# Attention ahead of an int8 linear layer: another order of the work before the first scores

## The chip, the cores and the metric

The kernel runs on one core of a Trainium2 chip. The metric is device time in microseconds (us), from the launch of the program to its end. Engines are TensorE (PE in the profile; its weight loads are PEld), VectorE (DVE), ScalarE (ACT), GpSimd (POOL) and SyncE (SP), which issues the DMA transfers. On-chip data lies in SBUF; matmuls write to PSUM, which has eight banks of 128 x 512 float32.

## What is computed

The input x has 8 batches of 512 channels by 1024 tokens; cond is a 0/1 mask of 8 x 1024. First comes masked self-attention with 16 heads of 32 channels, then a linear layer with int8 weights along the token axis, quantised by row, and the residual:

```python
Q, K, V = (proj(Wq), proj(Wk), proj(Wv))            # einsum 'oc,bct->bto', split into heads
att = einsum('bhqd,bhkd->bhqk', Q, K) / sqrt(32) + b[0]
att = softmax(att * m + (1 - m) * -1e30, axis=-1)   # m: the mask of the key
y = einsum('bhqk,bhkd->bhqd', att, V)               # back to (B, C, T)
scale = max(abs(y).max(-1), 1e-7) / 127
q = clip(round(y / scale), -128, 127).astype(int8)
out = x + (q @ weight.T * scale * w_scale + bias).astype(float16)
```

## The kernel before, in words

**Tiling.** Four heads (128 channels) of one batch are a group `i`; there are 32 groups. The 1024 tokens of the queries are two halves `h` of 512; a group and a half are `X` (64 of them). The keys go in eight chunks of 128. One step `s` of the main loop takes one X and one chunk: `scores(s)` (L408 on) computes the transposed scores of four heads into two PSUM tiles, ScalarE takes their exponentials (L433), GpSimd adds them up over the chunks (L445), and `product(s)` multiplies by v (L458). Scores are shifted by each query's largest score. The shift is the first operand that goes into a scores tile: a matmul of a block of ones with the tile `shift` (L419), after which the score matmuls accumulate (L424).

**Where the shift comes from.** One X ahead, `maxima(k)` computes the scores the other way round: one matmul pair per unit, a unit `k` being one X, one of four heads `j` and one of four blocks of 128 queries (16 units an X). VectorE reduces the 128 x 1024 result to one column (`take_maxima`, L376). The operands of these matmuls are stacks: 128 x 1024 tiles with the high and low parts of one head's q or k in four slabs of 32 rows, filled by DMA (`stack_head`, L322; four transfers of 64 KB for one head, one of q and k, and one half). When the 16 units of an X are reduced, `split_tops` (L395, L397, GpSimd) splits the column into three bfloat16 parts, and `place_tops` (L402) transposes them by DMA into `shift`.

**PSUM.** Pool `ps_s` (tag "s") has two tiles of two banks, used by the scores and by some maxima; `ps_m` (tag "m") one tile of two banks, for the other maxima; `ps_av` (tag "av") one bank for the product with v; `ps_job` (tag "job") one bank for projections and the linear layer. A tile is written again when its readers are done. `maxima_bank(k)` takes "s" for k mod 4 of 1 and 2, "m" for 0 and 3.

**The order.** It is written out by hand: each engine executes in program order, without a scheduler. The main loop runs over pairs of steps, `n`, with `i, p = divmod(n, 8)`. It starts at n = FIRST = -5; the pairs below 0 have no scores and prepare the first X. In each pair, `job(i, p)` returns a list of pieces of other matmul work (a projection of a later group, v, or the linear layer of an earlier one), which are dealt out between four maxima units, `jobs["bank"]` being the PSUM tile that they write. Where a pair has eight pieces, one of them is done as narrow matmuls (`columns`, L197) between the pair's two scores. What follows a pair (`flush(later)`, then `after_units`) stands behind it on the engines' streams: the low parts of q and k on VectorE, and the transfers on SP.

**Ahead of the pairs.** `first_projections` (L251 to L277) computes k of group 0 in a whole "s" tile, and q's first half in the "job" bank, chunk by chunk of the channels as x arrives; then it copies them to `full`, and makes high (ScalarE) and low parts (GpSimd). The first eight units are done from `full` by `first_maxima`, two units (heads 0 and 1) at a time (L363), in pairs -5 and -4. Units from 8 on need the stacks of heads 2 and 3, and X = 1 (units from 16, in pair -1) those of head 0 with q's second half.

The jobs of the pairs below 0, and what follows each:

| pair | job (eight pieces each) | stacks put on SP behind it, or at its start |
| --- | --- | --- |
| -5 | v of group 0, first half of the tokens | heads 2, then 3: k both halves, q first half |
| -4 | q of group 0, second half | head 0: k both halves, q second half |
| -3 | v of group 0, second half | |
| -2 | q of group 1, first half | |
| -1 | k of group 1, first half | at its start, behind the transpose: head 1 k both halves, heads 1, 2, 3 q second half |

The lines of pairs 1 and 2 (group 0, p = 1 and 2) in `job` give a quarter of v of group 1 each, four pieces; the linear layer of an earlier group, which fills these pairs later on, does not exist yet.

Of the kernel before, what the change touches and what calls it, by code (L numbers as in the profile page):

```python
# [9 lines left out]
F32 = mybir.dt.float32  # L10
# [10 lines left out]
P = 128  # L21
DH = 32
HG = P // DH
HALF = 512
QUARTER = 256
# [7 lines left out]
def kernel(  # L33
# [216 lines left out]

    def first_projections():  # L251

        pair = ps_s.tile([P, NH, HALF], F32, tag="s", name="kps_0")
        accs = [(1, 0, pair[:, 0, :]), (1, 1, pair[:, 1, :]), (0, 0, bank("qps_0"))]
        for c in range(NG):
            for which, h, acc in accs:
                nc.tensor.matmul(
                    acc,
                    w_qk[0, which][:, c, :],
                    x_sb[0, c][:, h * HALF : (h + 1) * HALF],  # L260
                    start=(c == 0),
                    stop=(c == NG - 1),
                )
        top = masks[0][1]
        for which, h, acc in accs:
            split_tiles(0, which, h)
            f = full[0, which, h]
            if which == 0:
                nc.scalar.activation(f, acc, AF.Copy, scale=top)
            elif h == 0:  # L270
                nc.vector.tensor_copy(f, acc)
            else:
                nc.scalar.copy(f, acc)
        for which, h, acc in accs:
            high, low = splits[0, which, h]
            nc.scalar.copy(high, full[0, which, h])
            nc.gpsimd.tensor_tensor(low, full[0, which, h], high.bitcast(F32), ALU.subtract)  # L277

    v_sb = {}

    def project_v(i, quarters):

        b, g = divmod(i, NG)
        KQ = QUARTER // P

        def piece(a, r, matmul=nc.tensor.matmul):
            if i not in v_sb:
                v_sb[i] = work.tile([P, NT, P], F32, tag="v", name=f"v_{i}", bufs=2)
            acc = jobs["bank"]
            t, part = divmod(r, 2)  # L290
            k = a * KQ + t
            place = (k - quarters[0] * KQ) * P
            for c in range(part * NG // 2, (part + 1) * NG // 2):
                matmul(  # L294
                    acc[:, place : place + P],
                    x_sb[b, c][:, k * P : (k + 1) * P],
                    wv_sb[:, c, g * P : (g + 1) * P],
                    start=(c == 0),
                    stop=(c == NG - 1),
                )  # L300
            if (a, r) == (quarters[-1], 2 * KQ - 1):
                nc.scalar.copy(  # L302
                    v_sb[i][:, quarters[0] * KQ : (a + 1) * KQ, :].rearrange("p k c -> p (k c)"),
                    acc[:, : place + P],
                )

        return [lambda *x, a=a, r=r: piece(a, r, *x) for a in quarters for r in range(2 * KQ)]
# [5 lines left out]
            [P, T], F32R, tag="qk"[which], name=f"{'qk'[which]}s_{i}_{j}"  # L313
        )

    def stack_head(i, j, which, h):
        order = ((0, 0, 1, 1), (0, 1, 0, 1))[which]
        if (i, j, which) not in stacks:
            stack_tile(i, j, which)
        s = stacks[i, j, which]  # L320
        for a, part in enumerate(order):
            nc.sync.dma_start(  # L322
                s[a * DH : (a + 1) * DH, h * HALF : (h + 1) * HALF].bitcast(F32),
                splits[i, which, h][part][j * DH : (j + 1) * DH, :].bitcast(F32),
            )
# [3 lines left out]

    def maxima_bank(k):  # L330

        pool, tag = (ps_s, "s") if k % HN in (1, 2) else (ps_m, "m")
        return pool.tile([P, NH, HALF], F32, tag=tag, name=f"mps_{k}")

    def maxima(k):
# [351 lines left out]
    def group(i):  # L687
        return 0 <= i < n_groups

    def job(i, p):  # L690


        if i == last:
            return linear(i - 2, p, (0,), HALF) if p < 2 else []
        if i < 0:
            if p in (3, 5):
                return project_v(0, (0, 1) if p == 3 else (2, 3))
            if p == 4:
                return project(0, 0, 1)
            return project(1, p - 6, 0)  # L700
        if p == 0:
            return project(i + 1, 1, 1)
        if p == 3:
            return project_v(i + 1, (2, 3))
        if p == 4:
            return project(i + 1, 0, 1)
        if p == 7:
            return project(i + 2, 1, 0) if group(i + 2) else []
        h, a = divmod({1: 0, 2: 1, 5: 2, 6: 3}[p], 2)
        pieces = linear(i - 2, h, (a,)) if group(i - 2) else []  # L710
        if p in (1, 2):
            pieces += project_v(i + 1, (a,))
        elif group(i + 2):
            pieces += project(i + 2, 0, 0, (a,))
        return pieces

    def after_units(i, p):

        flush(stores)
        if i == last:  # L720
            if p == 2:
                for step in range(5):
                    normalise(2 * i - 1, step)
            if p == 3:
                quantise(i - 1, 0)
            if p == 5:
                turn(i - 1)
                for step in range(5):
                    normalise(2 * i, step)
        elif group(i - 1):  # L730
            if p in (2, 3):
                normalise(2 * i - 1, 2 * p - 4)
                normalise(2 * i - 1, 2 * p - 3)

            if p == 4:
                normalise(2 * i - 1, 4)
            if p == 5:
                quantise(i - 1, 0)
            if p == 7:
                turn(i - 1)  # L740
        if group(i) and i < last:
            if p == 6:
                normalise(2 * i, 0)
                normalise(2 * i, 1)
            if p == 7:
                normalise(2 * i, 2)
        if p == 0 and group(i - 1):
            normalise(2 * i - 2, 3)
            normalise(2 * i - 2, 4)
        if i < 0 and p == 3:  # L750
            for which in (1, 0):
                for j in range(HG):
                    stack_tile(0, j, which)
            load_w(1, 1)
            for j in (2, 3):
                for which, h in ((1, 0), (1, 1), (0, 0)):
                    stack_head(0, j, which, h)
        if group(i + 1):
            b, g = divmod(i + 1, NG)
            if g == NG - 2 and p == 6 and b + 1 < B:  # L760
                load_mask(b + 1)
            if g == NG - 1 and b + 1 < B:
                if 1 <= p < 4:
                    prepare_mask(b + 1, p - 1)
                if p == 3:
                    load_x(b + 1, 0)
                if p == 4:
                    for c in range(1, NG):
                        load_x(b + 1, c)
        if p == 4 and group(i + 1):  # L770
            if group(i + 2):
                load_w(i + 2, 0)

            if i >= 0:
                for which, h in ((1, 0), (0, 0), (1, 1)):
                    stack_head(i + 1, HG - 1, which, h)
            for j in range(HG if i >= 0 else 1):
                if i < 0:
                    for h in range(NH):
                        stack_head(0, j, 1, h)  # L780
                stack_head(i + 1, j, 0, 1)
        if p == 1 and i >= 0 and group(i + 2):
            load_w(i + 2, 1)

        ahead = i + 1 + (p == 7)
        if p in (7, 0) and group(ahead) and ahead > 0:
            j = (0, 1)[p == 0]
            stack_head(ahead, j, 1, 0)
            stack_head(ahead, j, 0, 0)
            for j in {7: (), 0: (0, 1)}[p]:  # L790
                stack_head(ahead, j, 1, 1)
# [22 lines left out]
    for n in range(FIRST, n_pairs):  # L814
# [7 lines left out]
        if (n + 1) % HP == 0 and 0 <= n + 1 < n_pairs:  # L822
            split_tops((n + 1) // HP)
            place_tops((n + 1) // HP)
            if n == -1:
                for h in range(NH):
                    stack_head(0, 1, 1, h)
                for j in range(1, HG):
                    stack_head(0, j, 0, 1)
            if p == HN - 1 and i >= 0 and group(i + 1):  # L830
                for which, h in ((1, 0), (0, 0), (1, 1)):
                    stack_head(i + 1, 2, which, h)
# [17 lines left out]
        if p in (5, 6) and 0 <= i < last:  # L850
            half_denominators(2 * i, p - 5)
        if pieces:
            jobs["bank"] = bank(f"job_{n}")
        if n == n_pairs - 1:
            open_linear(last - 1, 1)
            run_linear(2)
# [20 lines left out]
        for a in range(HN):  # L877
# [3 lines left out]
            elif units:  # L881
                maxima(units[a])

            if a > 0 or len(pieces) > NG:
                for _ in range(-(-len(pieces) // (HN - a))):
                    pieces.pop(0)()
        flush(later)
# [64 lines left out]
```

## Time and profile before

| what | value |
| --- | --- |
| median of 3 runs | 2558.18 us (2558.08 to 2558.53) |
| the profiled execution | 2559.6 us |
| its span | 2557.8 us |
| TensorE busy in the span | 2506.1 us (98%) |
| GpSimd | 2242.7 us (88%) |
| VectorE | 1802.7 us (70%) |
| ScalarE | 1479.1 us (58%) |
| the first maxima matmul | 19.37 us from the span's start |
| the first scores matmul (pair 0) | 56.40 us |
| start of pair 1 | 67.51 us |

Times of instructions are counted from the start of the span. A line of the timeline gives start, length, engine, source line, operation, the tiles written and read, shapes and count, and in brackets how long the engine was idle before and what ended that. A line of the stages gives the stretch, its length, each engine's busy time (and count), the clock granted to TensorE, the share of the DMA engines' time, and GB/s. A busy TensorE is not the same as one at its peak, since matmuls are pipelined. An idle engine costs nothing where another one sets the end.

### The profile page before, as it was taken

The numbers are of one execution on the slowest core, as the hardware profiler recorded it, in microseconds if no ns is written. First come the engines' busy times: TensorE is split into PE (matmuls) and PEld (weight loads), VectorE is DVE, ScalarE is ACT, GpSimd is POOL, SyncE is SP. The second block draws the span as 40 slices with busy tenths as digits, with TensorE's granted clock in tenths as the row PEclk, the third lists the DMA queues.
The fourth block names the chain that finished last, engine by engine and source line by source line (L and its number), as shares of the span: only waits on it lengthen the run. The fifth ranks groups of instructions, "written<-read, shape, count | busy, mean of one in ns | idle before, by whom it ended". The sixth has DMA issues, their size and how long they took to land.

```text
span 2557.8 us, 50828 instructions
## 1 busy us (share of the span) xinstructions
PE 2506.1 (98%) x19425; PEld 1429.6 (56%) x19428; DVE 1802.7 (70%) x2893; ACT 1479.1 (58%) x1657; POOL 2242.7 (88%) x909
## 2 busy tenths in 40 slices
PE   7999999999999999999999999999999999999997
PEld 4555555555555555555555555555555555555532
DVE  4567677777777677776777777777677777777774
ACT  2556665565655555655656655566655566556554
POOL 1889899999999989998999999999999998999991
PEclk9999999999999999999999999999999999999999
DMA  4423433333333333334333343333433334333321
GB/s 129 107 69 80 119 76 82 82 104 98 90 79 93 105 82 89 79 93 109 82 84 95 81 118 77 80 85 94 114 84 75 85 96 109 84 82 80 80 70 44
DMA packets 225952, 228.09 MB, mean 89 GB/s; under 512 B 104368, under 2 KB 138160, under 8 KB 225712
## 3 DMA queue, kind: packets, MB, share of 16 engines
q1 hardware_dynamic: 225712, 224.85, 34.4%
q8 instruction: 156, 2.56, 0.4%
q14 instruction: 84, 0.69, 0.1%
HBM read 57.70 MB, written 16.78 MB: 29 GB/s over the span
## 4 chain that ended last, share of the span: by engine, by line
PE 79%; POOL 11%; DMA 3%; issue 2%; ACT 2%; DVE 1%; SPq 1%; POOLq 0%; DVEq 0%; ACTq 0%
PE mps L345 17%; PE av L458 15%; PE sps L424 14%; PE job L208 13%; POOL sum L445 10%; PE job L294 7%; PE sps L419 6%; PE job L635 3%; PE dps L474 2%; PE job L197 2%; DMA wq<-in_wqT 2%; ACT e L433 1%; DVE rest L376 1%; SPq L322 1%; DMA ks<-kl 1%
## 5 line engine op out<-in xcount | busy, mean ns | idle before, releaser
L445 POOL TENSOR_TENSOR sum<-sum,e 128x2048 f32<-128x2048 f32 x374 | 1706.7, 4563 | 39.1 <-ACT e L433 20.5
L376 DVE CUSTOM_DVE_ANT_0 rest<-mps,row 128x1024 bf16<-128x1024 f32 x1024 | 1254.2, 1225 | 620.0 <-PE mps L345 376.9
L433 ACT ACTIVATE e<-sps,kbias 128x1024 f32<-128x1024 f32 x1024 | 1085.8, 1111 | 453.7 <-PE sps L424 448.7
L345 PE MATMUL mps<-ks,qs 128*128 128x512 f32 x2032 | 764.9, 457 | 11.6 <-ACT e L433 8.1
L424 PE MATMUL sps<-qf,kf 32*128 32x512 f32 x4096 | 552.2, 590 | 0.0
L458 PE MATMUL av<-e,v 128*32 128x512 f32 x4096 | 493.4, 598 | 0.0
L345 PEld LDWEIGHTS mps<-ks,qs 128*128 128x128 f32 x2032 | 333.5, 190 | 238.8 <-DVE den L484 93.6
L445 POOL TENSOR_TENSOR sum<-e,e 128x2048 f32<-128x2048 f32 x63 | 286.2, 4542 | 154.8 <-ACT e L433 147.6
L458 PEld LDWEIGHTS av<-e,v 128*32 128x32 f32 x4096 | 107.5, 109 | 346.4 <-issue 346.1
L294 PEld LDWEIGHTS job<-wv,x 128*128 128x128 f32 x1860 | 255.0, 191 | 27.1
L208 PE MATMUL job<-x,wq 128*128 128x256 f32 x914 | 247.9, 380 | 10.8 <-DMA wq<-in_wqT 7.0
L294 PE MATMUL job<-wv,x 128*128 128x128 f32 x1860 | 257.1, 274 | 0.0
L419 PE MATMUL sps<-shift,ones_b 32*128 32x512 bf16 x2048 | 232.7, 383 | 5.9 <-DVE tops L376 3.0
L511 DVE RECIPROCAL den<-den 128x128 f32<-128x128 f32 x256 | 228.4, 925 | 0.0
L208 PE MATMUL job<-x,wk 128*128 128x256 f32 x854 | 223.8, 378 | 0.0
L424 PEld LDWEIGHTS sps<-qf,kf 32*128 32x128 f32 x4096 | 207.6, 184 | 4.3
L208 PEld LDWEIGHTS job<-x,wq 128*128 128x128 f32 x914 | 172.2, 189 | 47.7 <-DMA ks<-kl 8.4
L302 ACT COPY v<-job 128x256 f32<-128x256 f32 (+1 forms) x93 | 41.3, 444 | 252.5 <-PE job L294 252.5
L208 PEld LDWEIGHTS job<-x,wk 128*128 128x128 f32 x854 | 161.1, 189 | 30.9
L419 PEld LDWEIGHTS <-ones_b 32*128 32x128 bf16 x2048 | 70.6, 91 | 187.2 <-issue 169.6
L237 ACT ACTIVATE qh<-job,top 128x256 fp32r<-128x256 f32 (+1 forms) x91 | 49.8, 547 | 188.7 <-PE job L208 166.4
L635 PE MATMUL job<-w_sb,qT 128*128 128x256 bf16 (+1 forms) x942 | 125.9, 275 | 0.1
(101 smaller groups left out, 1438.4 us busy)
## 6 DMA issues: line engine op xcount, KB each, us to landing
ks<-kh SPq DMA_DIRECT2D x512, 64.0 KB, 2.0
ks<-kl SPq DMA_DIRECT2D x512, 64.0 KB, 2.0
qs<-qh SPq DMA_DIRECT2D x508, 64.0 KB, 2.0
qs<-ql SPq DMA_DIRECT2D x508, 64.0 KB, 2.0
x<-in_x SPq DMA_DIRECT2D x32, 512.0 KB, 6.0
xr<-in_x SPq DMA_DIRECT2D x64, 256.0 KB, 3.4
out<-o SPq DMA_DIRECT2D x64, 256.0 KB, 3.4
wk<-in_wkT SPq DMA_DIRECT2D x32, 256.0 KB, 3.7
```

Of the source, the lines that this page charges most:

```text
L197: nc.tensor.matmul(acc[r : r + DH], weights[:, r : r + DH], moving, **kwargs)
L208: matmul(acc[:, place], w[:, c, :], x_sb[b, c][:, h * HALF : (h + 1) * HALF][:, cols], start=(c == 0), stop=(c == NG - 1),)
L294: matmul(acc[:, place : place + P], x_sb[b, c][:, k * P : (k + 1) * P], wv_sb[:, c, g * P : (g + 1) * P], start=(c == 0), stop=(c == NG - 1),)
L345: nc.tensor.matmul(acc[:, a, :], q[:, n0 * P : (n0 + 1) * P], kk[:, a * HALF : (a + 1) * HALF], start=True, stop=True,)
L376: nc.vector.tensor_tensor_reduce(out=rest, in0=acc.rearrange("p h t -> p (h t)"), in1=row, scale=-1.0, scalar=HIGH, op0=ALU.add, op1=ALU.m ...
L419: nc.tensor.matmul(accs[j // 2][:, j % 2, :], ones_b[r, :], shift[r, :], start=True, stop=False)
L424: nc.tensor.matmul(accs[j // 2][:, j % 2, :], k[r, k0 * P : (k0 + 1) * P], q[r, :], start=False, stop=True,)
L433: nc.scalar.activation(e[:, 2 * a : 2 * a + 2, :], acc, AF.Exp, bias=kbias[:, kc : kc + 1], scale=SCALE)
L445: nc.gpsimd.tensor_tensor(sums[X], other, exps[s], ALU.add)
L458: nc.tensor.matmul(accs_av[X][r, :], v_sb[i][:, kc, r], exps[s][:, j, :], start=(kc == 0), stop=(kc == NT - 1),)
L511: nc.vector.reciprocal(piece, piece)
L635: matmul(acc, qT[:, k, :], w8_sb[:, k, half][:, cols], start=(k == 0), stop=(k == NT - 1),)
```

## The change

All of it lies ahead of pair 3.

- `first_projections` takes two "s" tiles, one for each half of k, in place of one. In the last chunk of channels, q's matmul comes first; ScalarE scales q before it copies k's second half.
- `maxima_bank`: units 0 to 19 (the pairs below 0) go by k mod 3: "m" for 1, "s" for 0 and 2, so the three tiles come round in turn.
- The jobs of the pairs below 0: q's second half over pairs -5 and -4, four pieces each, in one bank; v's first half in pair -3; group 1's q and k in -2 and -1 as before. v's second half is dealt to pairs 1 and 2, a quarter each, in the upper half of the bank (the `offset`) ahead of group 1's quarter. In the pairs below 0 a piece also follows the first of the four units in each case.
- The bank of these jobs is the "av" tile in pairs -3 and -1, the "job" tile otherwise.
- The stacks of head 3 are issued by ScalarE instead of SP. Head 0's k stack goes behind pair -5 on SP; head 1's k stack behind pair -4, after q's second half of head 0, in place of the start of pair -1.

```diff
-        pair = ps_s.tile([P, NH, HALF], F32, tag="s", name="kps_0")
-        accs = [(1, 0, pair[:, 0, :]), (1, 1, pair[:, 1, :]), (0, 0, bank("qps_0"))]
-        for c in range(NG):
-            for which, h, acc in accs:
+        k0, k1 = (ps_s.tile([P, HALF], F32, tag="s", name=f"kps_0_{h}") for h in range(NH))
+        accs = [(0, 0, bank("qps_0")), (1, 0, k0), (1, 1, k1)]
+
+        order = [(c, a) for c in range(NG - 1) for a in accs[1:] + accs[:1]]
+        order += [(NG - 1, a) for a in accs]
+        for c, (which, h, acc) in order:
...
-        for which, h, acc in accs:
+        for which, h, _ in accs[1:] + accs[:1]:
             high, low = splits[0, which, h]
...
-    def project_v(i, quarters):
+    def project_v(i, quarters, offset=0):
...
-            place = (k - quarters[0] * KQ) * P
+            place = offset + (k - quarters[0] * KQ) * P
...
-    def stack_head(i, j, which, h):
+    def stack_head(i, j, which, h, engine=nc.sync):
...
-        pool, tag = (ps_s, "s") if k % HN in (1, 2) else (ps_m, "m")
+
+        first = k < -FIRST * HN
+        pool, tag = (ps_s, "s") if (k % 3 != 1 if first else k % HN in (1, 2)) else (ps_m, "m")
...
         if i < 0:
-            if p in (3, 5):
-                return project_v(0, (0, 1) if p == 3 else (2, 3))
-            if p == 4:
-                return project(0, 0, 1)
-            return project(1, p - 6, 0)
+            if p < HP + 1:
+
+                if p == HP - 1:
+                    jobs["first"] = project(0, 0, 1)
+                return [jobs["first"].pop(0) for _ in range(NG)]
+            return project_v(0, (0, 1)) if p == 5 else project(1, p - 6, 0)
...
         if p in (1, 2):
+            if i == 0:
+
+                pieces = project_v(0, (NH + a,), QUARTER)
             pieces += project_v(i + 1, (a,))
...
-            for j in (2, 3):
+            for j, engine in ((2, nc.sync), (3, nc.scalar)):
                 for which, h in ((1, 0), (1, 1), (0, 0)):
-                    stack_head(0, j, which, h)
+                    stack_head(0, j, which, h, engine)
+            for h in range(NH):
+                stack_head(0, 0, 1, h)
...
             for j in range(HG if i >= 0 else 1):
-                if i < 0:
-                    for h in range(NH):
-                        stack_head(0, j, 1, h)
                 stack_head(i + 1, j, 0, 1)
+            if i < 0:
+                for h in range(NH):
+                    stack_head(0, 1, 1, h)
...
             if n == -1:
-                for h in range(NH):
-                    stack_head(0, 1, 1, h)
                 for j in range(1, HG):
                     stack_head(0, j, 0, 1)
...
         if pieces:
-            jobs["bank"] = bank(f"job_{n}")
+
+            if n < 0 and n % 2 and n > FIRST:
+                jobs["bank"] = ps_av.tile([P, HALF], F32, tag="av", name=f"job_{n}")
+            elif n != FIRST + 1:
+                jobs["bank"] = bank(f"job_{n}")
...
-            if a > 0 or len(pieces) > NG:
+            if a > 0 or len(pieces) > NG or n < 0:
                 for _ in range(-(-len(pieces) // (HN - a))):
                     pieces.pop(0)()
```

## The prediction

> **What bounds the kernel now.** I read the page first, then busy time by stage, then the timeline up to 100 us, the waits in it and the DMA issues.
>
> ```profile
> span 2557.8 us, 50828 instructions
> ...
> PE 2506.1 (98%) x19425; PEld 1429.6 (56%) x19428; DVE 1802.7 (70%) x2893; ACT 1479.1 (58%) x1657; POOL 2242.7 (88%) x909
> ...
> PE   7999999999999999999999999999999999999997
> ```
>
> TensorE is busy nearly everywhere: work on it costs its time, and only idle stretches can be won. They lie in the first slice, which is the stage that the change edits. By stage (the edges are the pairs' first matmuls; -5 and -4, then -3 to -1, then one pair a row from 0):
>
> ```profile
> core 0: us, PE busy (x) PEld busy (x) DVE busy (x) ACT busy (x) POOL busy (x), PEclk, DMA share, GB/s
> 19.37:36.47 17.10, 15.61 (x80) 9.32 (x80) 9.86 (x16) 2.81 (x6) 3.72 (x3) 1.00 0.36 87
> 36.47:56.40 19.93, 17.29 (x88) 14.08 (x89) 15.53 (x25) 2.39 (x4) 1.22 (x5) 1.00 0.31 79
> 56.40:67.51 11.11, 8.51 (x55) 5.16 (x56) 5.15 (x10) 5.32 (x6) 4.26 (x1) 1.00 0.40 97
> 67.51:76.76 9.25, 8.71 (x65) 4.62 (x64) 5.29 (x8) 5.32 (x6) 5.89 (x3) 1.00 0.67 189
> 76.76:86.17 9.41, 8.91 (x67) 4.74 (x67) 4.94 (x9) 4.62 (x5) 9.41 (x4) 1.00 0.47 122
> 86.17:97.11 10.94, 10.11 (x93) 6.52 (x93) 6.16 (x11) 5.20 (x6) 10.57 (x8) 1.00 0.22 54
> 97.11:106.90 9.79, 9.79 (x72) 5.61 (x73) 4.03 (x9) 4.72 (x5) 7.46 (x3) 1.00 0.35 89
> ```
>
> Pair 0 takes 11.11 us with 8.51 busy. VectorE has 9.86 and 15.53 us of work in 17.10 and 19.93. The timeline says where the chain waits:
>
> ```profile
> 27.95 1.99 PE L363 MATMUL mps<-kf,qf 32*128 32x512 f32 x8 [0.71 <-DVE tops L376]
> ...
> 36.47 0.73 PE L345 MATMUL mps<-ks,qs 128*128 128x512 f32 x2 [0.77 <-DVE tops L376]
> ...
> 48.45 1.23 DVE L376 CUSTOM_DVE_ANT_0 rest<-mps,row 128x1024 bf16<-128x1024 f32 x1
> ...
> 51.34 1.32 SPq L402 DMA_TRANSPOSE shift<-part  x1
> ...
> 56.40 0.40 PE L419 MATMUL sps<-shift,ones_b 32*128 32x512 bf16 x4
> ...
> 57.70 2.12 ACT L433 ACTIVATE e<-sps,kbias 128x1024 f32<-128x1024 f32 x2
> ...
> 62.46 0.70 PE L345 MATMUL mps<-ks,qs 128*128 128x512 f32 x2 [1.35 <-DMA qs<-ql]
> ...
> 97.11 0.39 PE L419 MATMUL sps<-shift,ones_b 32*128 32x512 bf16 x4 [0.83 <-DMA shift<-part]
> ```
>
> The maxima wait for tiles that VectorE still reads. The sixteenth reduction starts at 48.45 and ends at 49.7; the split and transpose follow, landing at 53.9 (2.5 us after issue, the median of the transposes). Scores start only at 56.40, since pair -1's matmuls stand ahead. Pair 0 then waits for a q stack queued on SP behind the transpose and eight k transfers.
>
> **The change, part by part.** The profiled execution took 2559.6 us, 1.8 around its span; it lies 1.4 above the median of 2558.18. I sum against it and carry the difference to the median.
>
> *First projections.* q's last matmul pair goes first and its scaling is ScalarE's first. In before k's copy started at 18.17 and q's scaling at 18.64, ending 19.32. Now q starts at 18.17 and ends at 18.85; the second k copy ends at 19.3, needed only by the later half of the first maxima. They start at 18.9, not 19.37: 0.5 won.
>
> *Pairs -5 and -4.* Each had two double maxima (1.92 us from start to next work, at 27.95 to 29.87) and eight projection pieces (1.9 per four): four steps of 3.84, 15.4 of the 17.1 us. Now a pair has four pieces, so a step is 1.92 + 0.96 = 2.88, and three tiles by turns leave the waits small: tile 3 needs reduction 0, done at 22.3 where TensorE comes at 21.8, but half of the double needs no wait; I count 0.2. Pair -3 starts at 18.9 + 4 x 2.88 + 0.2 = 30.6, not 36.47. VectorE starts a double's reductions 2.02 after its matmuls (27.95 to 29.97) and spaces them 1.375 (29.97 to 31.35): the eighth ends at 27.7 + 2.0 + 2 x 1.375 = 32.5.
>
> *Pairs -3 to -1.* A step (one maxima, two pieces) took TensorE 1.36 (38.73 to 40.08 to 41.44), under VectorE's 1.375, so VectorE sets the pace. After the eighth reduction comes q's low part (0.75), then eight reductions back to back: 33.35 + 11.0 = 44.35, not 49.7. The waits on one projection bank (0.65 and 0.90 ahead of the pieces at 37.85 and 51.37) go with two banks, already covered by that pace. Split and transpose as before, 4.2: shift lands at 48.4.
>
> *First scores.* Pair -1's third reduction must end before the second score tile has its bank: 44.35 + 0.75 + 3 x 1.375 + 0.05 = 49.25; TensorE's pieces end at 47.9 (the fourth maxima waits for the first reduction, 46.4, then 0.45 and two pieces). This wait takes the old one's place. From 49.25, 0.2 and 1.03 of score matmuls: exponentials start at 50.5, not 57.70: 7.2 won.
>
> *SP queue, pair 0.* The eight k transfers of head 1 go ahead of the transpose (from 0.63 x 8 = 5 us behind it) to behind q's second-half stack; SP is then done near 41, before the transpose at 45.9. After it four q transfers remain, landing near 51.2. The wait of 1.35 at 62.46 goes: TensorE comes to those maxima at 53.9. Total 7.2 + 1.3 = 8.5. The weight loads stay: the next q weights go out behind 20 stack transfers, near 33.1, landing at 36.4 (3.3), beside their use at 36.5.
>
> *Stacks of head 3 from ScalarE.* Twelve issues that SP took 0.59 each for (0.63 apart) go onto ScalarE's own stream at about 20.9, ahead of its next work, q's second half. No ScalarE issue is in the trace; nearest is the same transfer on SP, 0.59, the farthest is the transpose's 1.32, and nothing excludes less: 0.1 apiece changes no start here. I take 0.59: 20.9 + 12 x 0.63 = 28.5 (its last two wait for GpSimd's low part of q, 23.6 in before, so not longer), hidden, since q's second half is done only at 30.2 and VectorE takes its low part at 32.6. Above 0.87 the cover is gone and each further 0.1 moves the chain by 1.2. At 1.32 the cast starts at 36.7 and eight later reductions at 23.0 + 12 x 1.32 = 38.8: 5.5 of the 8.5 lost.
>
> *v in pairs 1 and 2.* 32 matmuls leave pair -3. Pairs 1 and 2 took 9.25 and 9.41 with four pieces; now they have eight, one narrow. Eight-piece pairs: 9.79 at pair 4, 10.11 busy in pair 3, 9.92 for pair 11 (164.30 to 174.22). By pair 11, the same v work without a wait: 2 x 9.92 - 18.66 = 1.2 lost; bounds 0.9 and 1.6. Little, because pairs 1 and 2 waited for exponentials there. One more v copy a pair is 0.37 of ScalarE, which is busy 5 of 9 us.
>
> *Pair 4.* Its shift waits behind GpSimd's sums, which run without a gap from 71.07 to 101.9, so it keeps its distance to pair 1's start while TensorE arrives 1.2 later: the 0.83 wait goes. Bounds 0 and 0.83.
>
> Sum: -8.5 + 1.2 - 0.8 = -8.1. From here the program is the same, and every engine's state is 8 to 8.5 us earlier, so it should last to the end: 2559.6 - 8.1 = 2551.5 by the profiled execution, 2558.18 - 8.1 = 2550.1 by the median.
>
> **The rivals.** 0.2% is 5.1 us, about what a measurement of this kernel can tell from no change.
>
> *The two queues slow each other.* The two lists run together from 20.9; if they take turns, each issue lasts about 1.2. ScalarE is free at 35.3, the later reductions start at 23.0 + 14.4 = 37.4 instead of 33.35, and 4.1 is lost: 2554.2. For it: only one queue's issues are in the trace.
>
> ```profile
> q1 hardware_dynamic: 4178, 4.19, 35.0%
> ...
> ks<-kh SPq DMA_DIRECT2D x16, 64.0 KB, 2.0
> ```
>
> Against: the DMA engines were 35% busy in that stretch. The Trainium skill, "DMA: Bandwidth & Descriptors", sections "Queues, rings and completion order" and "Issuing engines are not separate DMA queues", says that the two queues have neither DMA engines nor a descriptor generator of their own, and that issuing from several engines saves only sequencer time. By that rule, if the 0.59 is the generator's, this rival holds; if the sequencer's, the forecast. No run shows which. Chance 0.18.
>
> *Slower: ScalarE is held by its issues.* Same place, higher price: at t each, reductions restart at 23.0 + 12t. The 8.1 is used up where 12t = 33.35 + 8.1 - 23.0, t = 1.54; at 2.0 the kernel takes 2558.18 - 8.1 + 13.6 = 2563.7. For it: a copy's issue that had to wait stretches on SP too (1.32 at 29.36). Against: no unstretched issue of this kind exceeds 0.61. Chance 0.12.
>
> *The clock drops at the new gap.* Ahead of the first scores TensorE pauses 0.6 and again 0.6. One long pause in this trace, 2.17 us ahead of 892.85, was followed by
>
> ```profile
> 893.97:897.38 3.41, 3.41 (x12) 2.20 (x15) 2.18 (x3) 0.09 (x1) 3.41 (x1) 0.50 0.44 108
> ```
>
> half the clock for 3.41 us, while pauses of 1.70 and less were not. The price is at most 1.7: 2551.8. The Trainium skill, "TensorE: Matmul & The Clock Gate", Part 1, puts the drop after an idle window of about 3.4 us; the trace has it after less, so the row decides. Chance 0.08.
>
> **How the numbers follow.** Forecast 0.62 (own range 2549 to 2552.5), queues 0.18, slower 0.12, clock 0.08. Faster by over 0.2% (below 2553.1): 0.62 + 0.08 less 0.02 for issues a little above 0.87, 0.68. Within: the queues and those, 0.20. Slower: 0.12. The range goes from 2548.5 (v at 0.9, no tile waits, and the 0.70 that pair 0's narrow piece waited for its bank ahead of 58.36, which I count at nothing because the second scores wait for exponentials anyway, give 2548.9; a little is left under it) to 2556.0, past the queues' 2554.2, since an issue of 1.32 gives 2555.6; it leaves out the slower case and some low end.
>
> **What would show it.** Right: first double maxima at 18.9; pair -3 near 30.6; the sixteenth reduction ends near 44.4, with no VectorE gap after 33; transpose issue near 45.9; exponentials at 50.5; no DMA wait in pair 0, which ends near 59.0; pairs 1 and 2 near 9.9; no shift wait at pair 4; ScalarE's issues done by 29. Wrong: ScalarE issues above 0.87, a scaling of q after 31, reductions idle at 33 to 38, or a later stretch with waits that before lacked.

## The result, and the profile after

The changed kernel takes 2549.55 us (median of 12 runs, 2548.02 to 2554.53) where the kernel before, run beside it, takes 2557.30 (12 runs, 2553.84 to 2560.76). The ratio is 0.9973, with a 95% interval of 0.9965 to 0.998: faster by 0.27%, or 6.9 us (5.1 to 9.0). The forecast was 2550.1 and faster by more than 0.2%. The profiled execution took 2548.71 us.

The page of the changed kernel shows the same picture as before, with the first slice a little fuller:

```profile
span 2546.9 us, 50876 instructions
...
PE 2501.4 (98%) x19452; PEld 1429.1 (56%) x19452; DVE 1802.5 (71%) x2893; ACT 1479.2 (58%) x1658; POOL 2244.7 (88%) x909
...
PE   8999999999999999999999999999999999999997
```

The spans differ by 10.9 us, more than the change brought. In this execution the mask, whose preparation stands ahead of everything, had landed 1.25 us earlier (12.98 against 14.23 after the start), which no edit touches. The part from pair 4 to the end, where the programs are alike, took 2458.1 us here and 2460.7 in the execution before; over the profiled executions below it lies between 2454.7 and 2460.9. Apart from one of 6.92 us near the end, which both have, TensorE's pauses of over 0.2 us in that part add up to 21.5 us in this execution and to 18.0 in another of the same kernel; the longest of them are at the seven changes of batch, where it waits mostly for transfers. So a few microseconds are read from the stages, counted from the first maxima matmul (17.64 now, 19.37 before), and not from a span.

Busy time by stage, with the edges as in the table of before: pairs -5 and -4, then -3 to -1, then one pair a row from pair 0:

```profile
core 0: us, PE busy (x) PEld busy (x) DVE busy (x) ACT busy (x) POOL busy (x), PEclk, DMA share, GB/s
17.64:29.91 12.27, 12.27 (x48) 6.41 (x49) 8.39 (x13) 2.12 (x4) 3.72 (x3) 1.00 0.67 166
29.91:48.08 18.17, 16.66 (x90) 14.07 (x89) 16.23 (x28) 4.20 (x7) 1.23 (x5) 1.00 0.38 88
48.08:57.79 9.71, 8.53 (x54) 5.33 (x56) 5.72 (x12) 4.24 (x4) 2.87 (x1) 1.00 0.42 103
57.79:68.35 10.56, 10.10 (x93) 6.49 (x93) 5.76 (x10) 5.68 (x7) 8.61 (x3) 1.00 0.66 195
68.35:78.96 10.61, 10.15 (x93) 6.56 (x93) 4.93 (x9) 4.99 (x6) 10.53 (x5) 1.00 0.32 82
78.96:88.85 9.89, 9.89 (x93) 6.49 (x93) 4.80 (x9) 4.61 (x5) 9.52 (x8) 1.00 0.27 42
88.85:98.63 9.78, 9.78 (x71) 5.60 (x72) 4.92 (x9) 5.30 (x6) 6.11 (x2) 1.00 0.30 80
```

Pairs -5 and -4 went from 17.10 to 12.27, pairs -3 to -1 from 19.93 to 18.17, pair 0 from 11.11 to 9.71. Pairs 1 and 2 went the other way, from 9.25 and 9.41 to 10.56 and 10.61, more than forecast: TensorE was not busy for 0.46 us in each. Pair 3 lost its shift wait (10.94 to 9.89). The timeline of the changed kernel (the tile `job_-5_179` holds q's second half):

```profile
28.91 1.22 DVE L380 CUSTOM_DVE_ANT_0 rest<-mps,row 128x1024 bf16<-128x1024 f32 x1 [0.37 <-PE mps L367]
...
30.30 0.69 ACT L237 ACTIVATE qh<-job_-5_179,top 128x512 fp32r<-128x512 f32 x1 [10.54 <-DMA ks<-kh]
...
41.89 1.22 DVE L380 CUSTOM_DVE_ANT_0 rest<-mps,row 128x1024 bf16<-128x1024 f32 x1
...
44.80 1.32 SPq L406 DMA_TRANSPOSE shift<-part  x1
...
48.08 0.46 PE L423 MATMUL sps<-shift,ones_b 32*128 32x512 bf16 x4 [1.51 <-DMA shift<-part]
...
49.37 2.12 ACT L437 ACTIVATE e<-sps,kbias 128x1024 f32<-128x1024 f32 x2 [1.68 <-PE sps L428]
...
65.02 0.37 ACT L304 COPY v<-job 128x256 f32<-128x256 f32 x1 [0.27 <-PE job L296]
65.44 0.71 PE L296 MATMUL job<-wv,x 128*128 128x128 f32 x4 [0.46 <-ACT v L304]
```

The sixteenth reduction starts at 41.89 where it was 48.45; the seven ahead of it, from the ninth on, run back to back. The first scores wait 1.51 us, now for the transpose. In the last two lines, in pair 1, TensorE waits for a copy of v: the wait that I had not priced.

### The profile page after: what moved, and what is told of

Its sections match the earlier page's. It is cut to its first block, busy times and chain, and to the rows that moved or that the text cites. A ratio compares the mean times of both kernels' runs of the same rounds, so it can differ in the third digit from the quotient of the medians.

```text
span 2546.9 us, 50876 instructions
## 1 busy us (share of the span) xinstructions
PE 2501.4 (98%) x19452; PEld 1429.1 (56%) x19452; DVE 1802.5 (71%) x2893; ACT 1479.2 (58%) x1658; POOL 2244.7 (88%) x909
## 4 chain that ended last, share of the span: by engine, by line
PE 79%; POOL 12%; DMA 3%; issue 2%; ACT 2%; DVE 1%; SPq 1%; POOLq 0%; DVEq 0%; ACTq 0%
PE mps L349 17%; PE av L462 15%; PE sps L428 14%; PE job L208 13%; POOL sum L449 10%; PE job L296 7%; PE sps L423 6%; PE job L639 3%; PE dps L478 2%; DMA wq<-in_wqT 2%; PE job L197 2%; ACT e L437 1%; DVE rest L380 1%; SPq L324 1%; POOL o L623 0%
```

## The experiments

Each is the changed kernel with one edit. The table gives, from one profiled execution each, the time from the first maxima to the first scores, the lengths of the pairs, and the time from the first maxima to pair 4, behind which the programs are alike (starts of matmuls, subtracted; us).

| kernel | to the first scores | pair 0 | pairs 1 + 2 | pair 3 | to pair 4 |
| --- | --- | --- | --- | --- | --- |
| before | 37.03 | 11.11 | 18.66 | 10.94 | 77.74 |
| changed | 30.44 | 9.71 | 21.17 | 9.89 | 71.21 |
| changed, again | 30.41 | 9.71 | 21.17 | 9.89 | 71.19 |
| heads_sp | 38.05 | 10.92 | 21.18 | 9.88 | 80.03 |
| heads_act | 36.54 | 10.88 | 21.18 | 9.89 | 78.48 |
| tiles_old | 39.99 | 9.99 | 21.17 | 9.89 | 81.04 |
| tiles_late | 31.81 | 9.99 | 21.17 | 9.88 | 72.87 |
| one_bank | 33.01 | 9.72 | 21.17 | 9.89 | 73.80 |
| k1_late | 30.91 | 14.47 | 21.17 | 9.88 | 76.43 |
| v_back | 33.49 | 9.72 | 18.65 | 11.04 | 72.90 |
| late_copy | 30.59 | 9.71 | 19.72 | 9.89 | 69.91 |
| pool_low | 30.08 | 9.71 | 21.19 | 9.89 | 70.86 |
| late_pool | 30.08 | 9.71 | 19.72 | 9.89 | 69.40 |
| first_order | 29.93 | 9.90 | 21.17 | 9.89 | 70.89 |

Pairs 1 to 3 repeat to 0.02 us where no edit touches them, so there the table tells tenths apart. Ahead of them it does not: the first scores wait for the first transpose, which took 2.5 us in some of these executions and up to 3.6 in others, and in late_copy, whose edit lies behind them, they came 0.15 later than in the changed kernel. The device times of kernels run once are not used, since twelve runs of the changed kernel alone lie 6.5 us apart.

### Do the two queues slow each other, and does an issue hold ScalarE?

The changed kernel itself answers the first. Its timeline, where both queues issue at once:

```profile
23.22 0.59 SPq L324 DMA_DIRECT2D ks<-kh  x1
23.51 0.60 ACTq L324 DMA_DIRECT2D ks<-kh  x1
23.86 0.59 SPq L324 DMA_DIRECT2D ks<-kl  x1
24.16 0.61 ACTq L324 DMA_DIRECT2D ks<-kl  x1
```

Each queue keeps its 0.59 to 0.61, and these stack transfers land 1.9 to 2.3 us after issue, where SP alone had 1.9 to 2.0 at the same place in the kernel before. The Trainium skill, "DMA: Bandwidth & Descriptors", section "Issuing engines are not separate DMA queues", says that issuing from several engines saves only sequencer time; the trace agrees, and that time was worth having here.

heads_sp:

```diff
-            for j, engine in ((2, nc.sync), (3, nc.scalar)):
+            for j, engine in ((2, nc.sync), (3, nc.sync)):
```

> The changed kernel with head 3's twelve stack transfers back on SP, behind head 2's. In the changed kernel the first scores come 30.44 us after the first maxima (48.08 and 17.64). If SP's issue time is what the second queue took off the path: 24 issues of 0.63 end near 34, eight of head 0 near 39, so the q weights of group 1 land near 42.4 where pair -2 wants them at 35.8, and the transpose stands behind head 1's transfers; first scores near 52.5, that is 34.9 after the first maxima (4.5 more). If VectorE's pace hides the issues anyway, 30.4 as now.

Measured: 38.05, 7.6 more than the changed kernel. The place is as expected, and the price larger:

```profile
37.65 0.79 PE L349 MATMUL mps<-ks,qs 128*128 128x512 f32 x2 [1.01 <-DMA qs<-ql]
...
44.26 2.08 PE L208 MATMUL job_-2_330<-x,wq 128*128 128x256 f32 x4 [5.82 <-DMA wq<-in_wqT]
```

TensorE waits 5.82 us for the q weights behind SP's list, and from within that wait its clock is at half for 6.8 us (41.7 to 48.6). With SP alone the change lost its gain in this execution, pair 4 coming 2.3 later after the first maxima than in the kernel before; how much of that is the halved clock was not separated.

heads_act:

```diff
-            for j, engine in ((2, nc.sync), (3, nc.scalar)):
+            for j, engine in ((2, nc.scalar), (3, nc.scalar)):
```

> The changed kernel with the stacks of heads 2 and 3 both issued by ScalarE, 24 issues. The rival that ScalarE is held by its issues, tried at twice the number: 18.75 + 24 x 0.64 = 34.1 is when q's second half can be cast (30.30 now), VectorE's low part of q goes from 31.60 to 35.4, and every later reduction with it: first scores 3.8 later, 34.2 after the first maxima. If an issue holds only the queue and not the engine behind it, 30.4 as now.

Measured: 36.54, 6.1 more. ScalarE works in order, and its cast stands behind the whole list:

```profile
35.39 1.25 ACTq L324 DMA_DIRECT2D qs<-ql  x2
36.68 0.69 ACT L237 ACTIVATE qh<-job_-5_179,top 128x512 fp32r<-128x512 f32 x1 [16.27 <-DMA qs<-qh]
```

The ninth reduction came 20.2 us after the first maxima, not 14.6: 5.6 later instead of 3.8, since one issue had to wait for GpSimd's low part and two others took 2.47 together, where a pair takes 1.19. TensorE then waited 4.8 us, and within that wait its clock fell to half for 6.8. So the slower rival's mechanism exists; at 0.6 an issue, twelve stay under their cover and 24 do not.

### The tiles by turns

tiles_old:

```diff
-        pool, tag = (ps_s, "s") if (k % 3 != 1 if first else k % HN in (1, 2)) else (ps_m, "m")
+        pool, tag = (ps_s, "s") if k % HN in (1, 2) else (ps_m, "m")
```

> The changed kernel with the maxima's tiles by the old rule (k mod 4), all else as changed. If the tiles by turns keep VectorE fed: the third double waits for reduction 3 (1.85 us), and each four units after the eighth begin with a gap of 0.85 on VectorE; the sixteenth reduction ends 2.4 later and the first scores come 32.8 after the first maxima instead of 30.44. If the shorter TensorE work of pairs -5 and -4 alone made the gain, 30.5.

Measured: 39.99, 9.5 more, with the first wait where expected, ahead of the third double. Then something else happened. The line of the wait, and busy time in stretches behind it:

```profile
25.65 3.76 PE L367 MATMUL mps<-kf,qf 32*128 32x512 f32 x8 [1.31 <-DVE tops L380]
```

```profile
17.99:25.90 7.91, 6.59 (x26) 3.44 (x28) 4.93 (x8) 1.97 (x4) 3.72 (x3) 0.99 0.66 164
25.90:32.00 6.10, 6.10 (x14) 2.59 (x15) 2.43 (x4) 0.00 (x0) 0.00 (x0) 0.50 0.63 153
32.00:38.00 6.00, 5.31 (x13) 2.04 (x10) 2.50 (x6) 0.83 (x2) 0.00 (x0) 0.50 0.09 22
38.00:43.00 5.00, 5.00 (x21) 4.62 (x22) 3.12 (x5) 0.43 (x1) 0.00 (x0) 0.52 0.46 121
43.00:50.00 7.00, 6.55 (x39) 5.66 (x38) 5.13 (x9) 0.58 (x1) 0.00 (x0) 1.00 0.27 66
```

The granted clock is half from 25.7 on, for 17.07 us in all, and a double maxima takes 3.8 us instead of 2.0. A second kernel keeps the turns for the first eight units. tiles_late:

```diff
-        first = k < -FIRST * HN
+        first = k < 2 * HN
```

> The changed kernel with the old rule for the maxima's tiles from the ninth unit on, so that pairs -5 and -4 keep the tiles by turns and TensorE isn't idle there. If the first test of the tiles was made larger by the halved clock: the clock stays whole, the sixteenth reduction ends 0.85 later (26.3 after the first maxima instead of 25.47), and TensorE, which has 1.5 to spare ahead of the scores, is held 2.2 and 1.1 at the two doubled tiles: first scores 32.4 instead of 30.44. If the tiles themselves cost the 9.5 us of that test, 35 or more.

Measured: 31.81, 1.4 more, under the 2.0 expected; the sixteenth reduction ends at 26.24 (26.3 expected), and the clock stays whole through this part, although TensorE has a pause here that is as long as the one in tiles_old:

```profile
33.32 0.73 PE L349 MATMUL mps<-ks,qs 128*128 128x512 f32 x2 [1.31 <-DVE tops L380]
```

So in the later pairs the turns are worth 1.4 us up to the first scores and 1.7 up to pair 4. In the first two they keep TensorE from a pause after which, in the one execution of tiles_old, it ran at half speed; whether it would in every execution is not shown. How much of the 9.5 the clock took and how much the waits was not separated.

### Banks, SP's order, the first projections

one_bank puts all jobs of the pairs below 0 in the job bank:

```diff
-            if n < 0 and n % 2 and n > FIRST:
-                jobs["bank"] = ps_av.tile([P, HALF], F32, tag="av", name=f"job_{n}")
-            elif n != FIRST + 1:
+            if n != FIRST + 1:
```

> The changed kernel with all jobs of the pairs below 0 in the job bank. TensorE's pieces of pairs -3 and -1 wait for VectorE's low parts (2 us each), but VectorE's pace covers most of it: first scores 31.0 after the first maxima (0.6 more; between 0.3 and 1.1). If the wait were on the path in full, 33 or more.

Measured: 33.01, 2.6 more. TensorE waits 1.68, 0.21 and 1.73 for banks, 3.6 in all, and had 1.51 to spare ahead of the scores; 3.6 - 1.5 = 2.1 explains most of it. I had taken VectorE's pace for a cover over these pairs. It is one only to the size of that reserve, so the second bank was worth more than the nothing that I gave it.

k1_late:

```diff
-            if i < 0:
-                for h in range(NH):
-                    stack_head(0, 1, 1, h)
...
             if n == -1:
+                for h in range(NH):
+                    stack_head(0, 1, 1, h)
                 for j in range(1, HG):
```

> The changed kernel with head 1's eight k transfers put back behind the transpose. If SP's order is what took the DMA wait out of pair 0: the q stack of head 1 lands 5 us later, near 55.2, where TensorE wants it at 52.7, so pair 0 takes 12.2 instead of 9.71 and waits 2.5 for a DMA; the first scores stay at 30.4 after the first maxima. If the transfers were hidden anyway, 9.7.

Measured: pair 0 takes 14.47 where 12.2 was expected.

```profile
57.15 1.19 PE L349 MATMUL mps<-ks,qs 128*128 128x512 f32 x2 [1.25 <-DMA qs<-ql]
...
56.00:62.80 6.80, 5.65 (x13) 4.54 (x14) 2.47 (x4) 1.96 (x2) 4.51 (x1) 0.50 0.40 98
```

The DMA wait is there (1.25 us, in the timeline; 2.5 expected), and two more things. ScalarE's cast of group 1's k waited until 51.51 for a late transfer that still read the tile, which put the exponentials behind it to 52.47 and the second scores to a wait of 1.41. And the clock was halved for 6.8 us (the second line, a stretch). The wait for the transfer and the longer wait for the exponentials (1.41 against 0.57) make 2.1 us, so SP's order carries at least the 1.3 that it was forecast to be worth; the rest of the 4.8 was not separated from the halved clock. The first scores came 0.5 later than expected, behind a transpose that took 3.61 us.

first_order:

```diff
-        accs = [(0, 0, bank("qps_0")), (1, 0, k0), (1, 1, k1)]
-
-        order = [(c, a) for c in range(NG - 1) for a in accs[1:] + accs[:1]]
-        order += [(NG - 1, a) for a in accs]
+        accs = [(1, 0, k0), (1, 1, k1), (0, 0, bank("qps_0"))]
+        order = [(c, a) for c in range(NG) for a in accs]
...
-        for which, h, _ in accs[1:] + accs[:1]:
+        for which, h, _ in accs:
```

> The changed kernel with the first projections in the old order (k before q in the last chunk, and ScalarE's copy of k ahead of q's scaling). If that order is worth 0.5: the first maxima start 5.2 us after the mask has landed instead of 4.66 (the changed kernel; 5.14 in the kernel before), and everything behind follows unchanged. If ScalarE's mask work hides the order, 4.7.

Measured: 6.53 us from the mask's landing to the first maxima, worse than expected. In this execution the projections were late: TensorE's clock was whole only from 11.49 us on, where it was from 8.78 in the changed kernel, and they ended at 19.08 instead of 17.58, with ScalarE waiting for them. q stands last in line; its scaling ended at 19.81, and the first maxima started 0.78 after the projections. In four executions with the new order (heads_sp, v_back, late_copy, pool_low) the projections came last too, and there the first maxima started 0.01 to 0.02 after them. So the old order costs about 0.8 us where the projections come last; where the mask work does, only the kernel before shows it, with 5.14 against 4.66. Part of it came back, since this execution's first transpose took 2.51 us and not 3.14 (first scores 29.93 after the first maxima), so pair 4 was 1.55 later counted from the mask.

### What moving v costs

late_copy:

```diff
-                nc.scalar.copy(
-                    v_sb[i][:, quarters[0] * KQ : (a + 1) * KQ, :].rearrange("p k c -> p (k c)"),
-                    acc[:, offset : place + P],
-                )
+                dst = v_sb[i][:, quarters[0] * KQ : (a + 1) * KQ, :].rearrange("p k c -> p (k c)")
+                src = acc[:, offset : place + P]
+                if offset:
+                    later.append(lambda: nc.scalar.copy(dst, src))
+                else:
+                    nc.scalar.copy(dst, src)
```

> The changed kernel with ScalarE's copy of group 0's v quarter put behind all pieces of the pair (pairs 1 and 2). If the matmuls of group 1's quarter wait for that copy, since both lie in one bank and the copy stands behind two exponentials: pairs 1 and 2 together 19.9 instead of 21.17. If the second quarter's work itself costs it, 21.1.

Measured: 19.72 for the two pairs, 1.45 less, and pair 4 1.3 earlier. The stages of the two pairs have no idle TensorE left (0.46 us in each in the changed kernel), and its busy time in them fell by another 0.26 or so each:

```profile
59.27:69.10 9.83, 9.83 (x93) 6.41 (x93) 5.73 (x10) 5.31 (x6) 7.87 (x3) 1.00 0.69 198
69.10:78.99 9.89, 9.89 (x94) 6.49 (x94) 4.93 (x9) 4.88 (x6) 9.81 (x5) 1.00 0.39 99
```

In the changed kernel four pieces fill the upper half of a bank, and the next piece, which writes the lower half, waits for the copy of the upper one. I had expected that copy to be held up by the two exponentials ahead of it on ScalarE. The trace says otherwise: they are done, and ScalarE has been idle for 0.27 us when the copy starts at 65.02, since it waits for the fourth piece itself, which ends at 64.98. TensorE's wait of 0.46 is the length of the copy (0.37) and the handing over; the exponentials ahead of it add nothing here. The Trainium skill, "PSUM — Partial Sum Buffer", section "PSUM bank collisions raise a hardware error", says that a matmul must not write a bank while another engine reads it, so the order is needed as long as the copy stands there. No run here shows what would happen without it; the edit moves the copy.

v_back puts v's second half into pair -2 instead, a v piece behind each of that pair's pieces, in the av tile:

```diff
-    def project_v(i, quarters, offset=0):
+    def project_v(i, quarters, offset=0, key="bank"):
...
-            acc = jobs["bank"]
+            acc = jobs[key]
...
-            return project_v(0, (0, 1)) if p == 5 else project(1, p - 6, 0)
+            if p == 5:
+                return project_v(0, (0, 1))
+            if p == 6:
+                two = zip(project(1, 0, 0), project_v(0, (2, 3), key="bank2"))
+                return [x for pair in two for x in pair]
+            return project(1, p - 6, 0)
...
-            if i == 0:
-
-                pieces = project_v(0, (NH + a,), QUARTER)
...
+            elif n == -2:
+                jobs["bank"] = bank(f"job_{n}")
+                jobs["bank2"] = ps_av.tile([P, HALF], F32, tag="av", name=f"job_{n}_v")
```

> The changed kernel with v's second half not in pairs 1 and 2 but in pair -2, dealt out between that pair's pieces, in the av tile. VectorE paces pairs -3 to -1, so 4.2 us more of TensorE work there should show only in part: first scores 31.5 after the first maxima (1.1 more), pairs 1 and 2 together 18.7 instead of 21.17, pair 3 10.7 (its shift wait is back) instead of 9.89: pair 4 starts 70.7 after the first maxima instead of 71.21. If the work costs its full time ahead of the scores, 73.

Measured: pairs 1 and 2 take 18.65 as expected and pair 3 11.04 (10.7 expected), but the first scores come 3.05 later, not 1.1, so pair 4 is 1.7 later than in the changed kernel, where 0.5 earlier was expected. The 4.2 us of matmuls and 0.92 for the av bank, less the 1.51 to spare, are 3.6, the size of it if not the exact figure. It is the same oversight as in one_bank. Against this placement, v in pairs 1 and 2 is worth 1.7 as written, and 3.0 with late_copy (72.90 - 69.91).

### VectorE's chain, and both edits

pool_low:

```diff
+            if (i, which, h) == (0, 0, 1):
+                nc.gpsimd.tensor_tensor(
+                    low, full[i, which, h][:, cols], high.bitcast(F32), ALU.subtract
+                )
-            if which == 0:
+            elif which == 0:
```

> The changed kernel with the low part of q's second half (group 0) made by GpSimd from the copy in SBUF, not by VectorE from PSUM: 0.75 us less on VectorE between the eighth and the ninth reduction. If VectorE's chain sets the first scores: 29.7 after the first maxima instead of 30.44. If TensorE's pieces or a transfer do: 30.4.

Measured: 30.08, half of the gain expected. The ninth reduction comes 0.60 earlier (0.15 of the 0.75 had run beside VectorE's own spacing of its instructions) and the transpose is issued 0.60 earlier, but it lands 3.39 us after issue instead of 3.14. VectorE's chain is on the path, with the transpose's landing behind it.

late_pool has both edits, and the changed kernel ran again beside it:

> The changed kernel with both of the edits that helped: ScalarE's copy of group 0's v quarter behind all pieces, and q's second low part on GpSimd. If both add up: first scores 30.1 after the first maxima, pairs 1 and 2 together 19.7, pair 4 starts 69.6 after the first maxima (71.21 in the changed kernel): 1.6 us less than the changed kernel, which is less than the 5 us that the times can tell apart, so the stages decide. If the earlier first scores are lost in pair 0, 69.9.

> The changed kernel once more, beside the one above: pair 4 starts 71.2 after the first maxima, as before; the median 7 us under the kernel before.

Measured: 69.40 to pair 4, 1.8 under the changed kernel's 71.19, and 8.3 under the kernel before. In time, late_pool is at 0.9966 of the kernel before (0.9955 to 0.9978; median 2548.18, 7 runs) and the changed kernel at 0.9966 (0.9953 to 0.9978; median 2547.21, 5 runs, against 2556.01: 8.8 less, where 7 was expected). The times do not tell the two apart; the stages do, with the reservation that what follows pair 4 varies by more than their difference.

## Why the prediction was right, and where it was not

- **First projections**, 0.5: from the mask's landing to the first maxima it went from 5.14 to 4.66, 0.48. Right for this execution. Over the twelve executions with the new order it was 4.66 in eight, and 4.89 to 5.03 in the four in which the projections came last.
- **Pairs -5 and -4**: pair -3 was forecast 11.7 us after the first maxima, and came 12.27 after. In the second and the fourth double the second unit starts 0.33 late because it waits for its tile, 0.65 in all instead of 0.2, and the four pieces of a step took up to 1.06 instead of 0.96. The eighth reduction ended 13.87 after, as forecast (13.6) within 0.3.
- **Pairs -3 to -1**: sixteenth reduction 25.47 after the first maxima, where the forecast's 44.35 - 18.9 is 25.45. That they agree to 0.02 is luck: the eighth was 0.3 late, and from its end to that of the sixteenth it took 11.60 where 11.85 was counted. That VectorE paces them is right in the changed kernel; that work on TensorE there is therefore covered was right for 1.5 us only (one_bank, v_back).
- **First scores**: exponentials 31.72 after the first maxima, forecast 31.6. I had named the second score tile's bank as the last wait. The trace names the transpose, which landed at 47.95 after 3.14 us instead of 2.5; the reduction that frees the tile ended at 48.08. The two came within 0.15, so the size was right although the last releaser was another. In first_order, where that transpose took 2.51, the exponentials came 31.41 after, so the bank alone would have given nearly the same. The forecast's landing of the shift has a slip that changes nothing: 44.35 + 4.2 is 48.55, not 48.4, and the bank's 49.25 is later than both.
- **SP's order, pair 0**: 11.11 to 9.71, 1.40 won where 1.3 was forecast; no DMA wait.
- **ScalarE's issues**: 0.52 to 0.62 unstretched, the last done at 27.34, three microseconds ahead of the cast at 30.30. The value taken from SP's row held, and both rivals that priced it higher fell: two queues at once kept their issue times, and the list ended under its cover.
- **v in pairs 1 and 2**: this term failed. Forecast +1.2 with bounds 0.9 and 1.6; measured 21.17 - 18.66 = +2.5. I priced the two pairs by pair 11, which has as many pieces but only one copy, at its end. Here a copy stands between two quarters in one bank, and the pieces behind it wait 0.46 us in each pair. I had counted that copy as ScalarE's time (0.37), and not asked who waits for it. With the copy moved (late_copy) the two pairs cost +1.06, within the bounds.
- **Pair 4's shift wait**: forecast -0.8 with bounds 0 and 0.83, measured 10.94 to 9.89, -1.05. The wait is gone as forecast, and in late_copy too, where TensorE arrives only 1.06 later. What the term left out is that pair 3's busy time also fell, from 10.11 to 9.89, which puts the whole outside the bounds.
- **Sum**: counted from the mask's landing, pair 4 came 82.88 us after it in the kernel before and 75.87 in the changed one, -7.0 where -8.1 was forecast; the 1.3 too little for v, less the 0.25 of pair 3, is the difference. With the mask's 1.25 and the 2.6 of the part behind pair 4 this makes the 10.9 between the two spans. The medians differ by 7.75, and the interval of 5.1 to 9.0 holds both.
- **The clock** did not drop at the new pause of 1.51 us, as taken. It dropped ahead of pair 1 in four of the kernels above, so the rival was a real one. Its row was not the only one in the trace of before: a pause of 6.93 us ahead of 2544.53 has a drop too, of 6.83 us, near the end.

## What to carry to other kernels

When work moves into a stage, ask of its evacuation (the copy out of PSUM) what you ask of its matmuls: which instructions stand behind the copy and who waits for the bank, since a row with the same count of pieces can lack exactly that wait. When one engine paces a stage, write down how much the other has to spare at the stage's end; only that much can be added for nothing (1.5 us here, not the 4.2 that v_back put there). A second issuing engine is worth its place when its list ends before that engine's next work, and costs the rest of the list when it does not.

## What the runs showed of the hardware

- A short pause can cost much more than itself, but not every time. In tiles_old TensorE's granted clock fell to half at 25.71, right behind a pause of 1.31 us, and stayed there for 17.07 us, with one more pause of 0.69 in it. In heads_sp and heads_act it fell 3.3 and 4.1 us into waits of 5.82 and 4.80 us, and in k1_late at 55.92, after pauses of 1.90, 1.41 and 0.61 us and at the start of one of 1.25; there it was 6.83 us each. The pause of 1.31 us in tiles_late and those of 1.51 to 2.46 in the changed kernel had no such sequel. All these stretches are whole multiples of 3.41 us, and so are the distances between their starts within one execution: 25.71, 2138.56 and 2469.65 in tiles_old are 619 and 716 times 3.413 apart. The Trainium skill, "TensorE: Matmul & The Clock Gate", Part 1, tells of a free-running window of about 3.4 us; the lengths and the distances agree, while the pauses that sufficed are shorter than a window. Counted on that grid, TensorE was idle for 1.31 to 3.41 us of the window ahead of each drop up to 2500 us, but a window with 1.92 idle in the changed kernel (from 882.6) had none behind it. What else in the window decides was not tried.
- The first transpose lands 2.51 to 2.55 us after issue in eight of the thirteen kernels and 3.1 to 3.6 in five. In those five a packet of the queue that the page calls q14 instruction starts 1.3 to 2.0 us after the issue; in the eight it starts earlier than 0.6 or later than 2.2. The 896 transposes into `shift` of all fourteen traces bear it out: the 97 behind whose issue a packet of an instruction queue (q14 or q8) starts within 1.0 to 2.1 us all landed 2.89 us or more after issue, and of the other 799 (median 2.45) only 17 took that long. The link is close; no run here moved the packets to test it.
